# A four-layer graph network: a buffer for the last keys' adjacency, ScalarE in the late projections, and sums in one-bank tiles

## The chip, the core and the metric

One core of a Trainium2 chip runs one program. The metric is the device time of an execution in microseconds (us). The kernel before takes 3120.9 us, the median of 3 runs between 3119.28 and 3121.2 us.

The engines named below: TensorE (PE in the profile; PEld its weight loads), VectorE (DVE), ScalarE (ACT), GpSimd (POOL) and SyncE (SP). The last two mostly issue transfers here. Each engine works through a queue of its own in order, and waits where an instruction needs something of another engine or of a transfer.

## What is computed

Four layers stand on the same nodes: x is 2708 x 512, adj 2708 x 2708 with about 1% ones and a full diagonal, all in fp32. Each is `x = layernorm(x + layer(x))`. The change lies in layer 0:

```python
# layer 0, H = 4 heads of D = 128 features
Xw  = einsum('hnd,hde->hne', X by head, W)               # projection by head
f1, f2 = Xw @ V[:, 0], Xw @ V[:, 1]                      # two numbers per node and head
att = masked_softmax(sigmoid(f1 + f2.T) * adj, adj > 0)  # by head, n x n
Xc  = att @ Xw                                           # encoder
Xn  = batchnorm(Xc)
emb = batchnorm(elu(Xn @ Wm.T + bm) + Xn)                # mlp of the encoder
Y   = elu((att @ emb) @ W.T)                             # decoder, by head
out = batchnorm(elu(Y @ Wd.T + bd) + Y)                  # mlp of the decoder
```

Layer 1 is a mean over neighbours of `x @ W + b`, layer 2 an edge softmax times a node softmax, layer 3 an attention with the adjacency added to the scores twice. They follow in the same program, and the diff does not touch them.

## The kernel before

**Projection.** `project` takes the keys in blocks of 128 rows (22 blocks, `BLOCKS`, the last of 20). `values_of(jt)` multiplies block jt with all four heads' weights into a PSUM tile of two banks, `pxw`; its 512 wide part is copied to `xw` (L317, by ScalarE or VectorE, as the argument `scalar` says), and the column f2 is halved into `f2h` (L321, VectorE). The first 17 blocks are issued at once, with ScalarE for the first 14. The last five, 17 to 21, come in `rest`, which is called after the argument of step 1; ScalarE copies the first two of them. At the end of `rest` two small tiles are made: `bm1` (L343) and `enc_less` (L344).

**Encoder.** `encoder_pass` goes over 88 steps (`STEPS`): four parts of 22 blocks. A part is one half `hf` of the query nodes (1354 of 2708) and one pair `p` of heads; in order (0,0), (0,1), (1,0), (1,1). The block of 20 rows stands in the middle of a part, at place 11. For a step ScalarE makes two tanhs (L383, one for each head), VectorE joins them with the adjacency block `a` (`t`, 128 x 2708, the "argument", L378), ScalarE takes the exp (L515), and TensorE adds the result to 22 sums of up to 128 nodes each, 11 for a head (`node_sums`, L548; 44 records in the trace). The sums of three nodes share a bank with a column for the denominator each; the two heads use 4 banks each.

In the parts with p = 0 the block `a` comes from the input adjT (L480), VectorE turns zeros into -1e30 in two instructions (`mask_block`: z L443, a L444), and GpSimd writes the result to the DRAM tile `adj_d` (L448), from which the parts with p = 1 and the decoder load it. Steps up to a few are loaded ahead; `a` is a ring of 4 buffers (tag `a`). The block of 20 rows is not loaded as rows: its 20 x 1354 is cut into 4 strips of 384 columns, laid one below the other, with the gaps filled, by 7 transfers (`load_strips`, L430 to L435), into a buffer of the same ring; the strips of f1 go into `few` (L421).

**End of a part.** `keep` divides the sums by the denominators (rc L781, L782; rows L783, VectorE), and gives back two "turns", one for a head. A turn transposes the rows on TensorE (L802, L810) into banks, and the results are copied to `ft` (L823; columns 512, 512 and 330), by ScalarE or VectorE. The last bank also holds the transposed reciprocals; VectorE copies them to `sm`, 11 x 128 (L812), and GpSimd writes `sm` to the DRAM tile `rs_d` in two transfers (L814, L818). `sm` is taken from the pool `att` with the pool's own number of buffers, two. The turns are called within the first steps of the next part, and the exp of a step is issued behind the copies of the turn before it:

```python
if pending == 1:
    exponentials(k - 1, *copies_done)
```

**Mlp and decoder.** `mlp` normalises `ft` (L944, ScalarE, 452 or 450 columns each), multiplies four output groups in each of the six column chunks (L964), and applies elu (L701 ScalarE; L706, L708 VectorE), the sum with `ft` (L977) and statistics (L978). `decoder_pass` goes through the same four parts with the exps taken anew (L378, L635) or read back; its sums (`feature_sums`, L650) are six per part: two heads times three chunks of queries. At the end of a part VectorE reads them out (L1054).

**PSUM.** There are eight banks. For the encoder's sums they are eight tiles of one bank, four for a head; the turns of both heads transpose into the four of the second head (L802), so the next part's sums for that head start as these are copied out. The projection's, the decoder's six sums and the mlp's outputs use tiles of two banks with the tags `po0` to `po2`.

**Order.** The framework orders the instructions of each engine before the program runs, from the order they are written in, costs of its own and priorities; `behind(...)` adds a wish that one stands after another. It also places the waits: a tile's buffer is given to the next tile only after all its readers, transfers among them, are done. So a line moved, or a buffer fewer, can shift the place of others in the queues.

Of the kernel before, what the change touches and what calls it, by code (L numbers as in the profile page):

```python
# [29 lines left out]
def gnn_stack_kernel(  # L30
# [158 lines left out]
    with ExitStack() as l0:  # L189
# [45 lines left out]
        def project(att, psum):  # L235
# [66 lines left out]

            def values_of(jt, scalar):
                j0, n = BLOCKS[jt]
                pxw = psum.tile([P, H // HP, BANK], F32, tag=f"po{jt % HB}", name="pxw")
                pv = pxw[:, :, : HP * (P + 2)].rearrange("p a (k e) -> p a k e", k=HP)
                for h in range(H):
                    nc.tensor.matmul(
                        pv[:n, h // HP, h % HP, :],
                        xT_sb[:, h, j0 : j0 + n],  # L310
                        w0x[:, h, :],
                        start=True,
                        stop=True,
                    )

                copy = nc.scalar.copy if scalar else nc.vector.tensor_copy
                copy(  # L317
                    xw[:n, jt, :, :P].rearrange("p (a k) d -> p a k d", a=H // HP, k=HP),
                    pv[:n, :, :, :P],
                )  # L320
                nc.vector.tensor_scalar(  # L321
                    f2h[:n, jt, :].rearrange("p (a k) -> p a k", k=HP),
                    pv[:n, :, :, P + 1],
                    0.5,
                    None,
                    ALU.mult,
                )
            AT_ONCE = NT - 5
# [3 lines left out]
            def rest(step):  # L332

                with tc.issue_after(step.ins):
                    for jt in range(AT_ONCE, NT):
                        values_of(jt, jt < AT_ONCE + 2)
# [7 lines left out]
                    return nc.vector.tensor_scalar(  # L344
                        less, prm_sb[:, MB_ENC, :], 1.0, None, ALU.subtract
                    )

# [47 lines left out]
        def encoder_pass(values, att, banks, finish, f1b, blocks, spread, rest):  # L395

            FRONT, LEAD = 2, 2
            tanh, args, exps, tiles, loads, fetched, brought = ([] for _ in range(7))
# [65 lines left out]
            def bring(k):  # L464
# [6 lines left out]
                if k < len(blocks):  # L471
                    a = blocks[k]
                else:
                    a = att.tile([P, HW], F32, tag="a", name="a", bufs=4)
                    if n < P:
                        load_strips(a, src, hf)
                    else:
                        with behind(*[spread] if k < len(blocks) + 2 else []):
                            loads.append(
                                nc.sync.dma_start(a[:n, :w], src[j0 : j0 + n, h0 : h0 + w])  # L480
                            )
# [78 lines left out]
            for k in range(len(STEPS) + FRONT):  # L560
# [4 lines left out]
                if pending != 1 and 0 < k <= len(STEPS):  # L565
                    exponentials(k - 1)
                if inside and not pending:
                    form(k)
                    if k == 1:
                        args.append(rest(args[1]))  # L570
                        po = banks()
                if k >= FRONT:
# [32 lines left out]
        def decoder_pass(values, att, psum, finish):  # L605
# [53 lines left out]
            for part in PARTS:  # L659
                hf, p = part  # L660
                h0, w = HSPAN[hf]
                for place, jt in enumerate(ORDER):
# [20 lines left out]
                    if place == 0:  # L683
                        both = [
                            psum.tile([P, HP, BANK], F32, tag=f"po{q}", name="po", bufs=1)
                            for q in range(HB)
                        ]
                        po = [both[q][:, k, :] for k in range(HP) for q in range(HB)]
# [47 lines left out]
        with (  # L736
# [20 lines left out]
            def keep(hf, p, po, later):  # L757
# [35 lines left out]
                def turn(k, b, scalar, after):  # L793
# [15 lines left out]
                    if b + 1 == TURNS:  # L809
                        done = nc.tensor.transpose(bank[:NB, BANK - P :], rc, ident)  # L810
                        sm = att.tile([NB, P], F32, tag="sm", name="sm")
# [98 lines left out]
        with (  # L910
# [43 lines left out]
            for ci, (c0, w) in enumerate(CHUNKS):  # L954
# [3 lines left out]
                for o in range(C):  # L958
                    if o % HP == 0:
                        slot = (C * ci + o) // HP % HB  # L960
                        pair = psum.tile([P, HP, BANK], F32, tag=f"po{slot}", name="ps_mlp")
                    ps = pair[:, o % HP, :]
# [1314 lines left out]
```

## Time and profile before

| | us |
|---|---|
| median of 3 runs | 3120.9 |
| profiled execution | 3120.7 |
| its span, first to last instruction | 3118.8 |
| around the span | 1.9 |

The clock that TensorE was granted is 0.997 of full speed over the span. Where the stages lie, with the busy time of four engines in each:

| stage | us | PE | DVE | ACT | clock |
|---|---|---|---|---|---|
| projection | 0 to 41.7 | 32.1 | 21.9 | 22.2 | 1.00 |
| encoder, part 1 | 41.7 to 152 | 106.0 | 105.3 | 102.9 | 0.98 |
| first border | 152 to 165 | 11.2 | 12.7 | 10.6 | 1.00 |
| part 2 | 165 to 262 | 97.0 | 76.6 | 97.0 | 1.00 |
| second border | 262 to 278 | 13.5 | 15.7 | 12.3 | 0.89 |
| part 3 | 278 to 375 | 96.9 | 85.6 | 97.0 | 1.00 |
| third border | 375 to 388 | 11.3 | 12.9 | 10.4 | 1.00 |
| part 4 | 388 to 487 | 98.6 | 67.7 | 93.0 | 1.00 |
| last border, batch norm | 487 to 505 | 16.6 | 9.0 | 14.1 | 1.00 |
| mlp | 505 to 590 | 83.4 | 69.9 | 52.6 | 1.00 |
| decoder | 590 to 1030 | 435.7 | 306.8 | 324.9 | 0.99 |
| mlp of the decoder | 1030 to 1092 | 60.1 | 55.9 | 24.7 | 1.00 |
| layers 1 to 3 | 1092 to 3118.8 | 2008.3 | 1185.4 | 491.5 | 1.00 |

How to read it: busy time next to the length of the stage shows how much room an engine has left. An engine with room can still be late at one place, and the borders are such places: there the work of four engines depends on each other in a chain, while inside a part the next steps are prepared ahead. A gap of TensorE's is looked up in the list of what each engine waited for, which names the last instruction to come.

### The profile page before, as it was taken

The numbers are of one execution on the slowest core, as the hardware profiler recorded it, in microseconds if no ns is written. First come the engines' busy times: TensorE is split into PE (matmuls) and PEld (weight loads), VectorE is DVE, ScalarE is ACT, GpSimd is POOL, SyncE is SP. The second block draws the span as 40 slices with busy tenths as digits, with TensorE's granted clock in tenths as the row PEclk, the third lists the DMA queues.
The fourth block names the chain that finished last, engine by engine and source line by source line (L and its number), as shares of the span: only waits on it lengthen the run. The fifth ranks groups of instructions, "written<-read, shape, count | busy, mean of one in ns | idle before, by whom it ended". The sixth has DMA issues, their size and how long they took to land.

```text
span 3118.8 us, 39610 instructions
## 1 busy us (share of the span) xinstructions
PE 3070.6 (98%) x15144; PEld 2336.9 (75%) x15144; DVE 2025.3 (65%) x3804; ACT 1353.1 (43%) x1655; POOL 175.2 (6%) x301
## 2 busy tenths in 40 slices
PE   8999999999999999999999999999999999999999
PEld 7999996544444447875588887787778888888886
DVE  7988966785885783452366668677555555555565
ACT  7999998587767350001133334435211111111111
POOL 1111100000000000000111101000010000000000
PEclk9999999999999999999999999999999999999999
DMA  8987964266445315530254445566331111111110
GB/s 277 333 313 251 321 235 144 79 232 221 161 173 192 108 42 158 144 97 31 67 166 133 136 138 165 164 177 184 108 95 36 50 51 51 51 51 50 50 52 29
DMA packets 207228, 430.10 MB, mean 138 GB/s; under 512 B 22218, under 2 KB 137598, under 8 KB 201294
## 3 DMA queue, kind: packets, MB, share of 16 engines
q1 hardware_dynamic: 182774, 326.20, 34.0%
q0 software_dynamic: 24256, 101.35, 8.9%
q8 instruction: 119, 1.95, 0.3%
q14 instruction: 71, 0.58, 0.1%
q10 hardware_dynamic: 8, 0.02, 0.0%
HBM read 330.07 MB, written 95.87 MB: 137 GB/s over the span
## 4 chain that ended last, share of the span: by engine, by line
PE 79%; ACT 8%; DVE 8%; issue 3%; DMA 1%; SPq 0%; DVEq 0%; ACTq 0%; POOLq 0%
PE po L1728 21%; PE ps_s L1523 18%; PE po L650 9%; PE ps_nb L1326 7%; PE ps_wide L1376 5%; PE po L548 4%; ACT t L383 4%; ACT t L515 3%; DVE t L378 2%; PE ps_v L131 2%; PE ps_sup L1934 2%; PE ps_hid L131 2%; PE ps_dec L1093 2%; PE ps_mlp L964 1%; DVE a L444 1%
## 5 line engine op out<-in xcount | busy, mean ns | idle before, releaser
L378 DVE SCALAR_TENSOR_TENSOR t<-t,a 128x2708 f32<-128x2708 f32 (+1 forms) x152 | 443.8, 2922 | 166.1 <-ACT t L383 165.8
L548 PE MATMUL po<-xw,t 128*128 128x129 f32 (+2 forms) x3872 | 428.2, 277 | 11.8 <-DVE rc L781 4.9
L548 PEld LDWEIGHTS po<-xw,t 128*128 128x128 f32 (+2 forms) x3872 | 422.8, 189 | 16.4 <-issue 7.9
L383 ACT ACTIVATE t<-f1b,f2h 128x1354 f32<-128x1354 f32 x296 | 404.4, 1412 | 34.2 <-PE po L650 34.2
L1523 PE MATMUL ps_s<-q,hT 128*128 128x256 f32 (+1 forms) x1848 | 405.5, 372 | 0.0
L1728 PE MATMUL po<-sup,e 128*128 128x256 f32 (+1 forms) x1512 | 398.2, 384 | 5.6 <-DVE c L1809 2.8
L650 PE MATMUL po<-t,emb 128*128 128x452 f32 (+3 forms) x1056 | 399.1, 547 | 4.3 <-ACT t L635 4.2
L1523 PEld LDWEIGHTS ps_s<-q,hT 128*128 128x128 f32 x1848 | 339.5, 190 | 49.5 <-issue 5.1
L650 PEld LDWEIGHTS po<-t,emb 128*128 128x128 f32 (+1 forms) x1056 | 194.2, 191 | 202.1 <-issue 189.2
L1728 PEld LDWEIGHTS po<-sup,e 128*128 128x128 f32 (+1 forms) x1512 | 264.7, 185 | 59.6 <-issue 19.8
L1728 PE MATMUL po<-held,T 128*128 128x256 f32 x1200 | 293.8, 380 | 0.0
L1728 PEld LDWEIGHTS po<-held,T 128*128 128x128 f32 x1200 | 227.0, 190 | 31.1 <-issue 0.9
L2129 DVE SCALAR_TENSOR_TENSOR e<-a_cols,ps_s 128x512 f32<-128x512 f32 (+1 forms) x121 | 79.6, 658 | 233.8 <-PE ps_s L1523 229.9
L1523 PE MATMUL ps_s<-hT 128*128 128x256 f32 (+2 forms) x968 | 213.8, 372 | 0.8 <-ACT sup L1941 0.7
L515 ACT ACTIVATE t<-t 128x2708 f32<-128x2708 f32 x88 | 209.2, 2377 | 8.8 <-DVE t L378 8.1
L1523 PEld LDWEIGHTS ps_s<-hT 128*128 128x128 f32 x968 | 175.1, 190 | 29.1 <-issue 3.9
L1326 PE MATMUL ps_nb<-hid_hi,at 128*128 128x512 f32 x484 | 185.6, 390 | 0.4 <-DVE at L1318 0.4
L635 ACT ACTIVATE t<-t 128x2708 f32<-128x2708 f32 x64 | 157.3, 2458 | 60.4 <-DVE t L378 60.2
L1326 PE MATMUL ps_nb<-hid_lo,at 128*128 128x512 f32 x462 | 180.0, 390 | 0.0
L2031 ACT ACTIVATE a_score<-a_score,neg_big 128x512 f32<-128x512 f32 (+3 forms) x131 | 88.4, 683 | 196.0 <-DMA a_score<-in_adjT_dram 98.9
L2121 ACT ACTIVATE q<-ps_wide,uq 128x256 f32<-128x256 f32 (+1 forms) x44 | 20.5, 465 | 335.7 <-PE ps_wide L1376 335.7
L1633 ACT ACTIVATE e<-e 128x512 f32<-128x512 f32 (+1 forms) x187 | 113.8, 615 | 118.2 <-DVE e L1632 117.9
(276 smaller groups left out, 3995.4 us busy)
## 6 DMA issues: line engine op xcount, KB each, us to landing
a<-adj_d SPq DMA_DIRECT2D x113, 677.0 KB
a_cols<-in_adjT_dram SPq DMA_DIRECT2D x200, 256.0 KB
kept<-t POOLq DMA_DIRECT2D x20, 1354.0 KB, 8.4
t<-kept SPq DMA_DIRECT2D x20, 1354.0 KB
raw<-in_adjT_dram SPq DMA_DIRECT2D x105, 256.0 KB
a<-in_adjT_dram SPq DMA_DIRECT2D x37, 677.0 KB
adj_d<-a POOLq DMA_DIRECT2D x37, 677.0 KB, 6.2
a_score<-in_adjT_dram SPq DMA_DIRECT2D x55, 256.0 KB
```

Source lines behind the costliest of these rows:

```text
L131: nc.tensor.matmul(ps[:n], xt[:, c, :n], w[:, c, :], start=(c == 0), stop=(c == C - 1))
L378: return nc.vector.scalar_tensor_tensor(t, t, GUARD, ab, ALU.add, ALU.mult)
L383: done = nc.scalar.activation(t[:, k, :], f1b[k][:n, :w], AF.Tanh, bias=f2h[:n, jt, h : h + 1], scale=0.5,)
L515: nc.scalar.activation(t, t, AF.Exp, scale=0.5)
L548: nc.tensor.matmul(po[k][b][:m, s * DR : (s + 1) * DR], t[own : own + n, k, i0 : i0 + m], values[own : own + n, jt, HP * p + k, :], start= ...
L635: nc.scalar.activation(t, t, AF.Exp, scale=0.5)
L650: nc.tensor.matmul(po[HB * k + q][:, :qw], values[r : r + n, jt, h * P : (h + 1) * P], t[r : r + n, k, q0 : q0 + qw], start=(place == 0), ...
L1326: nc.tensor.matmul(pos[it][:n], at, half[:, jt, :], start=(jt == 0 and k == 0), stop=(jt == NT - 1),)
L1376: nc.tensor.matmul(ps[:, :width], w(c, o), xt(c), start=(c == 0), stop=(c == C - 1),)
L1523: nc.tensor.matmul(ps[:, jb, i:w], keys[:, c, j : j + P], st["q"][:, c, i:], start=(c == 0), stop=(c == C - 1),)
L1633: return nc.scalar.activation(e, e, AF.Exp)
L1728: nc.tensor.matmul(po[bank][rows, half, :], lhsT, rhs, start=(k == 0 and half == 0) if first is None else first, stop=last, skip_group_che ...
```

## The change

Four things, all in layer 0:

1. `values_of` and `rest`: of the late blocks 17 to 21 ScalarE copies three rather than two, and for those three it also writes the half of f2 (an activation, scale 0.5), which VectorE did. The exp of step 0 is issued after the last of these, rather than ahead of the argument of step 1.
2. The strips of the last block's adjacency get a tile of their own, `a_few` (one buffer, 384 columns), loaded at place 4 of each part behind the newest block load. The ring `a` is for full blocks alone.
3. `decoder_pass` and `mlp`: six tiles of one bank rather than three of two.
4. `sm` has one buffer rather than two.

```diff
--- before.py
+++ after.py
@@ -300,6 +300,8 @@
                 load_columns(NCH - 1)
                 nc.sync.dma_start(prm_sb, prm)
 
+            AT_ONCE, taken = NT - 5, []
+
             def values_of(jt, scalar):
                 j0, n = BLOCKS[jt]
                 pxw = psum.tile([P, H // HP, BANK], F32, tag=f"po{jt % HB}", name="pxw")
@@ -318,14 +320,13 @@
                     xw[:n, jt, :, :P].rearrange("p (a k) d -> p a k d", a=H // HP, k=HP),
                     pv[:n, :, :, :P],
                 )
-                nc.vector.tensor_scalar(
-                    f2h[:n, jt, :].rearrange("p (a k) -> p a k", k=HP),
-                    pv[:n, :, :, P + 1],
-                    0.5,
-                    None,
-                    ALU.mult,
-                )
-            AT_ONCE = NT - 5
+                half = f2h[:n, jt, :].rearrange("p (a k) -> p a k", k=HP)
+                if scalar and jt >= AT_ONCE:
+                    taken.append(
+                        nc.scalar.activation(half, pv[:n, :, :, P + 1], AF.Copy, scale=0.5)
+                    )
+                else:
+                    nc.vector.tensor_scalar(half, pv[:n, :, :, P + 1], 0.5, None, ALU.mult)
             for jt in range(AT_ONCE):
                 values_of(jt, jt < 2 * NT // 3)
 
@@ -333,7 +334,7 @@
 
                 with tc.issue_after(step.ins):
                     for jt in range(AT_ONCE, NT):
-                        values_of(jt, jt < AT_ONCE + 2)
+                        values_of(jt, jt < AT_ONCE + 3)
                     h0, w = HSPAN[1]
                     for q, (q0, _) in enumerate(HCH[1]):
                         f1_rows(HB + q, later_rows[:, q0:], q == 0)
@@ -341,9 +342,10 @@
                     copies(xw[:, NT - 1].rearrange("p h e -> p (h e)"))
                     copies(f2h[:, NT - 1, :])
                     nc.vector.tensor_scalar(bm1, prm_sb[:, MB_DEC, :], 1.0, None, ALU.subtract)
-                    return nc.vector.tensor_scalar(
+                    last = nc.vector.tensor_scalar(
                         less, prm_sb[:, MB_ENC, :], 1.0, None, ALU.subtract
                     )
+                return last, taken[-1]
 
             return f1b, blocks, spread, rest
 
@@ -395,7 +397,7 @@
         def encoder_pass(values, att, banks, finish, f1b, blocks, spread, rest):
 
             FRONT, LEAD = 2, 2
-            tanh, args, exps, tiles, loads, fetched, brought = ([] for _ in range(7))
+            tanh, args, exps, tiles, loads, fetched, brought, few = ([] for _ in range(8))
             state = {"f1b": f1b}
 
             def rows_of(k):
@@ -470,15 +472,18 @@
                 src = adjT if prepare else adj_d
                 if k < len(blocks):
                     a = blocks[k]
+                elif n < P:
+                    a = few.pop()
                 else:
                     a = att.tile([P, HW], F32, tag="a", name="a", bufs=4)
-                    if n < P:
-                        load_strips(a, src, hf)
-                    else:
-                        with behind(*[spread] if k < len(blocks) + 2 else []):
-                            loads.append(
-                                nc.sync.dma_start(a[:n, :w], src[j0 : j0 + n, h0 : h0 + w])
-                            )
+                    with behind(*[spread] if k < len(blocks) + 2 else []):
+                        loads.append(
+                            nc.sync.dma_start(a[:n, :w], src[j0 : j0 + n, h0 : h0 + w])
+                        )
+                if STEPS[k][1] == 4:
+                    few.append(att.tile([P, FEW], F32, tag="a_few", name="a_few", bufs=1))
+                    with behind(loads[-1]):
+                        load_strips(few[0], src, hf)
                 last_load[:] = loads[-1:]
                 if prepare:
                     mask_block(a, hf, jt, rows, width, *args[-1:])
@@ -562,13 +567,15 @@
                 copies_done = []
                 if inside:
                     open_step(k)
-                if pending != 1 and 0 < k <= len(STEPS):
+                if pending != 1 and 1 < k <= len(STEPS):
                     exponentials(k - 1)
                 if inside and not pending:
                     form(k)
                     if k == 1:
-                        args.append(rest(args[1]))
+                        done, scalar_done = rest(args[1])
+                        args.append(done)
                         po = banks()
+                        exponentials(0, scalar_done)
                 if k >= FRONT:
                     part, place = STEPS[k - FRONT]
                     t, _ = tiles[k - FRONT]
@@ -681,11 +688,10 @@
                         if p == 0 and jt in KEPT[1]:
                             count(hf, jt, att)
                     if place == 0:
-                        both = [
-                            psum.tile([P, HP, BANK], F32, tag=f"po{q}", name="po", bufs=1)
-                            for q in range(HB)
+                        po = [
+                            psum.tile([P, BANK], F32, tag=f"po{b}", name="po", bufs=1)
+                            for b in range(HP * HB)
                         ]
-                        po = [both[q][:, k, :] for k in range(HP) for q in range(HB)]
                     feature_sums(part, place, t)
                 later += finish(hf, p, po, rb) or []
             for work in later:
@@ -808,7 +814,7 @@
                     cw = min(w, c0 + BANK) - c0
                     if b + 1 == TURNS:
                         done = nc.tensor.transpose(bank[:NB, BANK - P :], rc, ident)
-                        sm = att.tile([NB, P], F32, tag="sm", name="sm")
+                        sm = att.tile([NB, P], F32, tag="sm", name="sm", bufs=1)
                         nc.vector.tensor_copy(sm, bank[:NB, BANK - P :])
                         full = (NB - 1) * P
                         nc.gpsimd.dma_start(
@@ -956,10 +962,8 @@
                     normal(ci + 1)
                 pss = []
                 for o in range(C):
-                    if o % HP == 0:
-                        slot = (C * ci + o) // HP % HB
-                        pair = psum.tile([P, HP, BANK], F32, tag=f"po{slot}", name="ps_mlp")
-                    ps = pair[:, o % HP, :]
+                    slot = (C * ci + o) % (HP * HB)
+                    ps = psum.tile([P, BANK], F32, tag=f"po{slot}", name="ps_mlp")
                     for c in range(C):
                         nc.tensor.matmul(
                             ps[:, :w],
```

Lines after the change stand 2 to 7 further down: L378 becomes L380, L515 L520, L548 L553, L812 L818, L823 L829, L650 L657.

## The prediction

> **What bounds the kernel.** I read the page's engine table first, then the groups, then TensorE's waits of the first 1100 us (the change ends there), then one window of the encoder, and last the timeline where the edits act.
>
> ```profile
> span 3118.8 us, 39610 instructions
> ...
> PE 3070.6 (98%) x15144; PEld 2336.9 (75%) x15144; DVE 2025.3 (65%) x3804; ACT 1353.1 (43%) x1655; POOL 175.2 (6%) x301
> ...
> L378 DVE SCALAR_TENSOR_TENSOR t<-t,a 128x2708 f32<-128x2708 f32 (+1 forms) x152 | 443.8, 2922 | 166.1 <-ACT t L383 165.8
> L548 PE MATMUL po<-xw,t 128*128 128x129 f32 (+2 forms) x3872 | 428.2, 277 | 11.8 <-DVE rc L781 4.9
> ...
> L515 ACT ACTIVATE t<-t 128x2708 f32<-128x2708 f32 x88 | 209.2, 2377 | 8.8 <-DVE t L378 8.1
> ```
>
> ```profile
> PE po L650 <- ACT t L635: 4.2, 4, 3.3
> PE po L548 <- ACT t L515: 3.9, 1, 3.9
> ...
> PE po L548 <- DVE enc_less L344: 1.5, 1, 1.5
> ...
> PE tp_emb L983 <- DVE ft L977: 1.4, 4, 0.6
> ```
>
> ```profile
> 130.00:260.00 130.00, 128.24 (x1172) 127.04 (x1171) 107.85 (x89) 127.20 (x82) 14.39 (x26) 1.00 0.88 327
> ```
>
> TensorE is 98% busy, so a gain can only be one of its gaps: the waits list (total, times, longest) names 3.9, 1.5 and some 1.4 us that the change touches. The third fence is decisive the other way: from 130 to 260 us ScalarE (fourth busy time) works 127.2 of 130 us, as hard as TensorE (128.2). A step of the encoder costs TensorE 4.91 us (44 records of L548) and ScalarE 4.98 us (distance of exps L515 from 174.72 to 199.62 us, five steps). So a delay of ScalarE inside a part is never made up, and reaches the end of the part whole.
>
> **Part one, the start (late projections on ScalarE).** The timeline has the last argument step L378 end at 37.99 and enc_less, which TensorE's first sum waits for, at 41.74. In between VectorE does three wide copies L317 (0.59 from start to start), four or five small ones (0.07 to 0.15), two f_later copies (0.59) and one wait. One wide copy and the halves of f2h go: 0.59 + 3 x 0.15 = 1.04. I take -1.1, bounds -1.5 (the whole wait) and 0. ScalarE gets 0.47 + 3 x 0.2 = 1.1 us ahead of exp 0 (35.13 to 36.2); that is hidden, since its exp 2 stands 2.2 us idle for VectorE; uncovered it would cost the 1.1 back.
>
> **Part two, the strips' own buffer.** In the old ring the load of a full block waits for the slot of a block behind:
>
> ```profile
> 94.95 0.87 DVE L443 TENSOR_SCALAR z<-a 128x1354 bf16<-128x1354 f32 x1 [1.70 <-DMA a<-in_adjT_dram]
> ...
> 97.33 2.97 DVE L378 SCALAR_TENSOR_TENSOR t<-t,a 128x2708 f32<-128x2708 f32 x1
> ...
> 100.34 2.46 ACT L515 ACTIVATE t<-t 128x2708 f32<-128x2708 f32 x1 [2.32 <-DVE t L378]
> ...
> 102.85 0.58 PE L548 MATMUL po<-xw,t 128*128 128x129 f32 x1 [3.92 <-ACT t L515]
> ```
>
> The bracket is the idle time before: 1.70 us of VectorE for a load issued at 87.46, right after a write of adj_d landed (87.41). With the strips out of the ring the load may use the slot freed at 79.84, so it is issued 7 us earlier and the wait goes: -1.75 (with its issue), bounds 0 (if another transfer takes the place) and -2.5. The 28 strip transfers are as many as before but earlier: seven issues of 0.36 us, 2.5 us of SP's queue per part, past which one block load is pushed; block loads here are issued 7 us ahead, so it is hidden. Parts one and two together: -2.85.
>
> **Part three, six one-bank tiles.** Decoder: the largest gap, 3.3 us at 793 us, ends with exp L635 (793.95 to 796.41; TensorE starts 796.44). The pair it would need is read out by 796.29, so freeing banks singly gains nothing: 0. One read-out now stands on VectorE ahead of an argument step; its bank is complete at 789.4, and VectorE is idle from 787.8 to 790.9, so that is hidden, and would cost 0.6 without the hole. Bounds -0.5 and +0.6. Mlp: the ScalarE order of the changed kernel puts five of the 21 normalisations (0.655 us from start to start) behind the first elu L701, so VectorE's chain, idle 5.3 us until then, starts 3.3 earlier. TensorE's gaps for ft there sum to 2.8 us in the timeline (the four in the list, 1.4, are the longest). I take -2.0, bounds -3.3 and 0.
>
> **Part four, sm in one buffer.** This is small in the diff and it decides. Head 1's sm (L812) now cannot be written before both rs_d writes of head 0's sm have landed, and the order of the changed program puts one more argument step ahead of it.
>
> ```profile
> DMA to landing us min/median/max: 1.6/4.1/7.8
> ```
>
> ```profile
> 387.58 0.27 DVE L812 COPY sm<-po 11x128 f32<-11x128 f32 x1
> 387.78 2.96 DVE L378 SCALAR_TENSOR_TENSOR t<-t,a 128x2708 f32<-128x2708 f32 x1
> 387.89 0.43 ACT L823 COPY ft<-po 128x330 f32<-128x330 f32 x1 [1.20 <-DVE sm L812]
> ...
> 388.22 2.46 ACT L515 ACTIVATE t<-t 128x2708 f32<-128x2708 f32 x1
> 388.38 5.40 PE L548 MATMUL po<-xw,t 128*128 128x129 f32 x46 [0.47 <-ACT ft L823]
> ```
>
> The first fence is the view of the tile sm (its eight pairs of writes), the second the timeline of the third border: sm at 387.58; 0.3 us later ScalarE's last ft copy, which waits for it; behind that in ScalarE's queue the exp of the next step, then all later tanhs. The same three start within 0.7 us of each other at the borders at 164, 277 and 388 us. Border one: sm moves behind the argument step (164.31 to 167.27), +3.0; writes landed at 165.8, in time. Border two: VectorE is busy throughout, the same 2.96 goes ahead of sm, +3.0. Border three: the writes land at 392.4 and 392.9 (7.7 us: a kept write of 1354 KB, issued at 381.92, is ahead of them in POOL's queue), so sm goes from 387.58 to 392.9, +5.3; bounds +3.0 (the argument step alone) and +5.3. The last border: second sm at 493.92, writes landed 493.75: +0.2. From this goes what the exps then had in hand, at most 0.1 at the ends of parts. Sum of the four: +11.4.
>
> On DMA, the Trainium skill (DMA: Bandwidth & Descriptors, "Anatomy of one DMA — SWDGE (gpsimd) path") gives a fixed cost of about 2.0 us per transfer, these being 5 KB. With that figure border three would be +3.0, the sum 2.3 us less; the trace's own 1.6 to 7.8 us decides.
>
> Who waits for whom else: TensorE needs the bank of that ft copy, but the new order has it 17 of 22 sums into the step rather than 7 to 12, so TensorE idles about 2, 2.5 and 4 us rather than 0 to 0.5. Idle time of 2.07 us (263.6 to 265.9) was followed by 3.4 us at half clock, 3.3 us at 793 by 6.8, 1.5 by none. Half of 3.4 is 1.7 us; of it about 1.3 is made up over 20 steps of 0.07 us, since TensorE then runs behind exps that are ready. Three borders at 0.4 to 0.7: +1.5, bounds 0 and +5.
>
> The skill's page TensorE: Matmul & The Clock Gate ("Why this matters for your kernels") asks for no gap over about 3 us; by it only border three pays, and the term would be about +0.5. The row at 263 us shows a shorter gap paying.
>
> **Sum.** -2.85 + 0 - 2.0 + 11.4 + 1.5 = +8.05 on the profiled execution: 3118.8 of span and 1.9 around it, 3120.7, gives 3128.75. The median of the runs is 0.2 above the profiled one, their spread 1.9. Forecast **3128.6**; its own range, from the bounds of border three and the clock, 3124 to 3133. A difference under 0.2% (6.2 us) could not be told from none.
>
> **Rivals.** (1) ScalarE passes sm: the copy finds its bank free without it, or sm slips in early, and the borders cost nothing. For it: at border two the bracketed wait is missing from the list for sm. Against: at all four borders the copy starts 0.03 us after sm's end. Gain: -2.85 - 2.0 and up to -2.4 for a gap at 265 us that the new order shortens: 3113.5. It is faster as soon as the borders cost less than 1 us together. Chance 0.11. (2) The borders cost one argument step each and no more, the writes land in time and the clock stays: 3 x 2.96 - 4.85 + 0.2 = +4.2, 3125; not slower by the bound. For it: writes landed after 1.6 us at 492. Chance 0.20. (3) The clock: each border's idle time brings 6.8 us at half speed as at 795 us, 2.9 us less work each, little made up: +4 to +6 over the forecast, 3134. For it 793 us; against 98 us, where 3.9 idle brought 3.4. Chance 0.13. (4) The gap at 793 us closes after all, with its slow clock: -3.3 - 3.0, 3122.3. Against: its exp keeps its place in ScalarE's order. Chance 0.06. The forecast keeps 0.50, of which a tenth lies within the bound. So faster 0.11, within 0.2% 0.20 + 0.06 + 0.05 = 0.31, slower 0.45 + 0.13 = 0.58. The range 3116 to 3135 leaves out most of rival 1 and the top of 3.
>
> **What would show it.** Argument L378 with no wait near 95 us and TensorE's first sum near 40.6: parts one and two. Sm's second copies behind an argument step, and the waits list with ft L829 after sm as a new top entry: part four; if the exp after each border stands less than 2.5 us later relative to the border's start, it is wrong. Gap at 793 us unchanged: part three. PE clock digits below 1 at the borders: the clock term. The forecast falls if the old ring's slots, and not sm, set ScalarE at the borders.

## The result, and the profile after

The changed kernel takes 3127.44 us (median of 12 runs, 3125.13 to 3129.1), the kernel before beside it 3118.86 us (12 runs, 3116.02 to 3121.6). The ratio is 1.0026 with a 95% interval of 1.0017 to 1.0035: slower by some 8.6 us. The profiled execution took 3126.81 us with a span of 3125.0, 6.1 us over the profiled one before.

Where the time goes is read from the start of the same sum on TensorE in both traces (every 44th record of the encoder, every 48th of the decoder), after minus before:

| place | after minus before, us |
|---|---|
| first sum of the encoder | -1.75 |
| step 12, behind the late block load | -3.42 |
| step 22, before the first border | -3.43 |
| step 43, before the second border | +0.92 |
| step 67, before the third border | +3.57 |
| last sum of the encoder | +6.83 |
| last sum of the mlp | +6.45 |
| decoder: 2/11, 5/11 and 1/2 through | +9.63, +8.75, +5.28 |
| last sum of the decoder | +6.45 |

So the encoder's first part gains 3.4, its three inner borders cost 4.35, 2.65 and 3.26, and the rest ends nearly even: the mlp takes 0.55 back, and the decoder moves up and down by some 3 us and ends where it began. ScalarE's exps (L515 before, L520 after), compared in the same way, shift by the same 4.35, 2.65 and 3.26 at the three borders: what the sums lose there is what the exps come late. The list of TensorE's waits in the first 1110 us (total, times, longest) has the new entry on top:

```profile
PE po L553 <- ACT ft L829: 6.2, 3, 2.7
...
PE po L657 <- ACT t L642: 4.5, 7, 2.0
PE po L553 <- DVE rc L787: 4.3, 3, 1.4
PE po L553 <- ACT t L520: 3.0, 2, 2.2
PE po L553 <- DVE enc_less L345: 1.9, 1, 1.9
...
PE tp_emb L987 <- DVE ft L981: 1.7, 2, 0.9
```

The first border in the timeline (start, us, engine and line; in brackets the idle time before and what ended it), in the kernel before:

```profile
161.23 2.96 DVE L378 SCALAR_TENSOR_TENSOR t<-t,a 128x2708 f32<-128x2708 f32 x1
...
164.11 0.27 DVE L812 COPY sm<-po 11x128 f32<-11x128 f32 x1
164.31 2.96 DVE L378 SCALAR_TENSOR_TENSOR t<-t,a 128x2708 f32<-128x2708 f32 x1
164.42 0.43 ACT L823 COPY ft<-po 128x330 f32<-128x330 f32 x1 [0.58 <-DVE sm L812]
```

In the changed kernel:

```profile
157.80 5.85 DVE L380 SCALAR_TENSOR_TENSOR t<-t,a 128x2708 f32<-128x2708 f32 x2
...
159.34 1.07 ACT L829 COPY ft<-po 128x512 f32<-128x512 f32 x2 [1.86 <-PE po L808]
...
165.03 0.28 DVE L818 COPY sm<-po 11x128 f32<-11x128 f32 x1 [1.38 <-DMA rs_d<-sm]
165.34 0.43 ACT L829 COPY ft<-po 128x330 f32<-128x330 f32 x1 [4.93 <-DVE sm L818]
...
165.67 2.46 ACT L520 ACTIVATE t<-t 128x2708 f32<-128x2708 f32 x1
...
165.83 3.59 PE L553 MATMUL po<-xw,t 128*128 128x129 f32 x16 [1.98 <-ACT ft L829]
```

The second and the third border of the changed kernel:

```profile
276.38 2.96 DVE L380 SCALAR_TENSOR_TENSOR t<-t,a 128x2708 f32<-128x2708 f32 x1
...
279.27 1.55 DVE L446 SCALAR_TENSOR_TENSOR a<-z,a 128x1354 f32<-128x1354 bf16 x1
...
280.75 0.27 DVE L818 COPY sm<-po 11x128 f32<-11x128 f32 x1
...
281.06 0.43 ACT L829 COPY ft<-po 128x330 f32<-128x330 f32 x1 [3.83 <-DVE sm L818]
```

```profile
388.13 5.85 DVE L380 SCALAR_TENSOR_TENSOR t<-t,a 128x2708 f32<-128x2708 f32 x2
...
394.41 0.28 DVE L818 COPY sm<-po 11x128 f32<-11x128 f32 x1 [0.43 <-DMA rs_d<-sm]
394.72 0.43 ACT L829 COPY ft<-po 128x330 f32<-128x330 f32 x1 [4.47 <-DVE sm L818]
```

Read them from the top. At the first and the third border two arguments now run together (x2, 5.85 us) where there was one ahead of sm and one behind. Then VectorE stands idle for another 1.38 or 0.43 us, ended by a transfer: the write of head 0's sm. All that time ScalarE waits (4.93 and 4.47 us) with the exp behind it. At the second border sm starts at 280.75, behind one argument more than before and the masks, with no idle time for the transfer (head 0's writes had landed at 277.50); ScalarE waits 3.83.

### The profile page after: what moved, and what is told of

It is laid out like the page before. It is cut to its first block, busy times and chain, and to the rows that moved or that the text cites. A ratio compares the mean times of both kernels' runs of the same rounds, so it can differ in the third digit from the quotient of the medians.

```text
span 3125.0 us, 39602 instructions
## 1 busy us (share of the span) xinstructions
PE 3072.0 (98%) x15144; PEld 2339.9 (75%) x15144; DVE 2024.7 (65%) x3800; ACT 1354.4 (43%) x1659; POOL 176.2 (6%) x301
## 4 chain that ended last, share of the span: by engine, by line
PE 77%; ACT 9%; DVE 8%; issue 4%; DMA 2%; POOL 0%; SPq 0%; DVEq 0%; ACTq 0%; POOLq 0%
PE po L1732 21%; PE ps_s L1527 19%; PE po L657 9%; PE ps_nb L1330 7%; PE ps_wide L1380 5%; ACT t L385 4%; ACT t L520 4%; DVE t L380 3%; PE ps_v L131 2%; PE ps_sup L1938 2%; PE ps_dec L1097 2%; PE ps_hid L131 2%; PE po L553 2%; PE ps_mlp L968 1%; PE ps_e L1660 1%
## 5 line engine op out<-in xcount | busy, mean ns | idle before, releaser
L380 DVE SCALAR_TENSOR_TENSOR t<-t,a 128x2708 f32<-128x2708 f32 x148 | 439.8, 2975 | 178.8 <-ACT t L385 178.5
L553 PE MATMUL po<-xw,t 128*128 128x129 f32 (+2 forms) x3872 | 431.9, 278 | 16.5 <-ACT ft L829 6.2
L553 PEld LDWEIGHTS po<-xw,t 128*128 128x128 f32 (+2 forms) x3872 | 423.7, 189 | 24.3 <-issue 8.3
L657 PE MATMUL po<-t,emb 128*128 128x452 f32 (+3 forms) x1056 | 397.5, 546 | 5.2 <-ACT t L642 4.5
L657 PEld LDWEIGHTS po<-t,emb 128*128 128x128 f32 (+1 forms) x1056 | 193.8, 190 | 202.6 <-issue 188.1
L520 ACT ACTIVATE t<-t 128x2708 f32<-128x2708 f32 x88 | 209.4, 2380 | 4.3 <-DVE t L380 3.5
```

Source lines behind the costliest of these rows:

```text
L380: return nc.vector.scalar_tensor_tensor(t, t, GUARD, ab, ALU.add, ALU.mult)
L520: nc.scalar.activation(t, t, AF.Exp, scale=0.5)
L553: nc.tensor.matmul(po[k][b][:m, s * DR : (s + 1) * DR], t[own : own + n, k, i0 : i0 + m], values[own : own + n, jt, HP * p + k, :], start= ...
L657: nc.tensor.matmul(po[HB * k + q][:, :qw], values[r : r + n, jt, h * P : (h + 1) * P], t[r : r + n, k, q0 : q0 + qw], start=(place == 0), ...
```

## The experiments

All ratios are to the kernel before, run on the same chip beside them. A ratio is estimated from all runs, so that it can differ from the quotient of the two medians by up to 0.0004; medians of different rows are best compared through their ratios.

| run | median, us | before, us | ratio | 95% interval |
|---|---|---|---|---|
| e1_sm_two | 3115.94 | 3120.01 | 0.9986 | 0.9977 to 0.9995 |
| e2_sm_one | 3129.52 | 3120.01 | 1.0030 | 1.0019 to 1.0041 |
| e3_banks | 3119.82 | 3120.01 | 1.0001 | 0.9992 to 1.0009 |
| e6_late | 3117.66 | 3120.01 | 0.9994 | 0.9985 to 1.0002 |
| e10_order | 3123.89 | 3119.05 | 1.0017 | 1.0008 to 1.0026 |
| e9_rs_sp | 3131.29 | 3119.05 | 1.0038 | 1.0026 to 1.0051 |
| e5_few | 3117.90 | 3119.05 | 1.0000 | 0.9991 to 1.0008 |
| e4_enc_sm_two | 3116.23 | 3119.05 | 0.9993 | 0.9983 to 1.0002 |
| e12_sm_behind | 3121.06 | 3119.47 | 1.0007 | 0.9999 to 1.0016 |
| e11_tanh | 3194.34 | 3119.47 | 1.0238 | 1.0225 to 1.0252 |

### Is it sm? Both ways round

e1_sm_two gives sm a second place: head 1's sm takes the tile of the f1 strips, which is free at the borders:

```diff
-                        sm = att.tile([NB, P], F32, tag="sm", name="sm", bufs=1)
+                        if k:
+                            sm = att.tile([P, HP, FEW], F32, tag="few", name="sm", bufs=1)[:NB, 0, :P]
+                        else:
+                            sm = att.tile([NB, P], F32, tag="sm", name="sm", bufs=1)
```

> The changed kernel, but head 1's sm in a buffer of its own (it borrows the tile of the f1 strips, free at the borders). Theory (one buffer of sm costs the borders 4.3 + 2.6 + 3.3 + 0.2 us, as the two traces show, and what is left is a small gain): 10 us less than the changed kernel, 3117, ratio to before 0.999 (0.998 to 1.000); the exp after each border starts within 1 us of where it stood relative to the border before. Rival (the borders are late for the strips' or the banks' sake, sm only happens to be there): the time stays at 3127, ratio 1.0026.

The other way round, the kernel before with this one line changed:

```diff
-                        sm = att.tile([NB, P], F32, tag="sm", name="sm")
+                        sm = att.tile([NB, P], F32, tag="sm", name="sm", bufs=1)
```

> The kernel before with nothing changed but one buffer for sm. Theory: all of the loss is here, +9 to +12 us, ratio 1.003 to 1.004, above what the whole change costs, since its gains are missing; each of three borders shows an argument step or a landing ahead of sm. Rival (ScalarE passes sm, or the loss needs the new order of the strips): within 0.05% of before.

Both came as the theory had it: ratio 0.9986 instead of 1.0026, and +9.5 us for the one line. In e1_sm_two the difference of the sums to before is the same on both sides of every border (-0.17 us at steps 22, 24 and 43, -0.16 at 45, -0.15 at 67, -0.14 at 68). Its waits of TensorE from 150 to 400 us:

```profile
PE po L553 <- DVE rc L787: 4.7, 3, 2.1
PE po L553 <- ACT ft L832: 0.9, 2, 0.5
```

The entry of 6.2 us is back at the 0.9 that the kernel before has. In e2_sm_one the exps come 2.89, 2.66 and 4.28 us later at the three borders. So sm is the loss, and the rest of the change is a gain of about 4 us by the medians: e1_sm_two is faster than both kernels. (Its trace shows less, since the profiled execution, 3118.98, is the slowest of its 11.)

### The argument ahead, or the landing?

One buffer brings two things: the scheduler puts an argument ahead of sm, and sm waits for the landing. e10_order has the first alone: two places for sm, but the turn is written behind the argument.

```diff
                     if turns:
+                        if inside and pending == 1:
+                            form(k)
                         scalar = pending == 1 or part[1] == 0
...
-                if inside and pending:
+                if inside and pending > 1:
```

> The changed kernel with two places for sm (as in e1_sm_two), but head 1's turn is written behind the next step's argument, so that VectorE has the order of the changed kernel without its wait for the writes. Theory (a border costs the argument step that is ahead, 2.96 us, and the landing only what comes on top): +3.0 us at the first and third border, +2.6 at the second, against e1_sm_two; sum +8.6, 3124.5, ratio to before 1.0015 (1.0005 to 1.0025). Rival (the landing alone makes the delay; the argument is moved into time that is lost anyway): within 2 us of e1_sm_two, 0.9990.

Measured 1.0017, as expected. Its first border:

```profile
156.88 5.84 DVE L380 SCALAR_TENSOR_TENSOR t<-t,a 128x2708 f32<-128x2708 f32 x2
...
162.65 0.27 DVE L823 COPY sm<-po 11x128 f32<-11x128 f32 x1
162.96 0.43 ACT L834 COPY ft<-po 128x330 f32<-128x330 f32 x1 [3.46 <-DVE sm L823]
```

The same two arguments, and sm directly behind them with no transfer in the bracket: ScalarE waits 3.46 us, 2.88 more than the 0.58 of the kernel before. From step 22 to the end of the encoder its sums go from -4.35 to +3.97 us against before: 8.3 us at three borders. The exps give 2.89, 2.65 and 2.77 for the single ones: an argument's 2.96 at each, less what the exps had in hand. The changed kernel has 1.46 more at the first border, none at the second and 0.49 at the third, close to what its sm waits there for the transfer (1.38, none, 0.43).

e9_rs_sp aims at the landing: SyncE issues the writes.

```diff
-                        nc.gpsimd.dma_start(
+                        nc.sync.dma_start(
```

(for both writes of sm)

> The changed kernel with one buffer for sm, its rs_d writes issued by SyncE instead of GpSimd. In this build the argument stays behind sm at the first and third border; sm still waits for the writes. Theory (what is left is the landing beyond the 3.1 to 3.8 us between the two sm): if SyncE's writes land in 2 to 5 us, each border costs 0 to 1.5 us, the second 2.6 (its argument is still ahead), sum 3 to 5, 3120, ratio 1.000 (0.999 to 1.001). Rival (any wait for a write at this place costs the 3 to 4 us seen, whoever issues it): 3127, 1.0026.

The theory's number fell: 3131.29, more than the changed kernel. The wait on the transfer is there, and longer:

```profile
157.95 1.31 SPq L820 DMA_DIRECT2D rs_d<-sm  x1
...
159.31 0.91 SPq L824 DMA_DIRECT2D rs_d<-sm  x1
...
165.18 0.28 DVE L818 COPY sm<-po 11x128 f32<-11x128 f32 x1 [4.77 <-DMA rs_d<-sm]
165.49 0.43 ACT L829 COPY ft<-po 128x330 f32<-128x330 f32 x1 [5.42 <-DVE sm L818]
...
165.98 4.24 PE L553 MATMUL po<-xw,t 128*128 128x129 f32 x18 [4.03 <-ACT ft L829]
```

With one argument fewer ahead of it sm still starts only at 165.18. SyncE issues the two writes 1.1 and 2.5 us after head 0's sm is done (GpSimd in the changed kernel: 0.3 and 0.8), and sm starts 5.9 us after the second issue (7.0 there): later issued and sooner done, it comes 8.6 us after head 0's sm rather than 8.1. So the two parts do not add up: sm goes when the later of the two is done. In the changed kernel the argument's 2.96 us lie inside the landing at the first and third border, and the landing adds 1.38 and 0.43 (the brackets above).

The exps come 4.84, 2.49 and 3.52 us later at the three borders, little more than in the changed kernel. The sums show 7.01, 0.33 and 6.01: at the first and the third border TensorE stood 4.0 us for the bank, 18 and 12 records into the step (32 in the changed kernel), and then had 6.8 us at half speed:

```profile
165.20:172.00 6.80, 6.02 (x28) 6.02 (x29) 4.20 (x3) 6.51 (x5) 0.00 (x0) 0.50 0.33 106
```

(the column behind POOL's busy time is the clock, 0.50.) The two together put the sums 2.2 and 2.5 us behind their exps; the first was made up by the second border, the other was not. It is what the prediction's third rival describes, and 2.5 of the 3.1 us by which the three borders cost more here than in the changed kernel.

### Through which wait does it reach the path?

e12_sm_behind keeps one buffer, but writes sm behind ScalarE's copy out of the same bank.

```diff
                         done = nc.tensor.transpose(bank[:NB, BANK - P :], rc, ident)
+                    dst = ft[:, h, h0 + c0 : h0 + c0 + cw]
+                    with behind(*after):
+                        copied = copy(dst, bank[:, :cw])
+                    if b + 1 == TURNS:
                         sm = att.tile([NB, P], F32, tag="sm", name="sm", bufs=1)
...
-                    dst = ft[:, h, h0 + c0 : h0 + c0 + cw]
-                    with behind(*after):
-                        copied = copy(dst, bank[:, :cw])
```

> The changed kernel, still one buffer for sm, but sm is written behind ScalarE's copy of 330 columns out of the same bank instead of ahead of it. Theory (the loss is ScalarE standing behind sm, through the bank that both read): the exps after the borders are no longer late; TensorE, which needs that bank 17 sums into the step, still waits for sm, 1 to 2.5 us at each of three borders, and makes up about 1.3 of it in each part: 0 to +4 us against e1_sm_two, 3118, ratio to before 0.9995 (0.9985 to 1.0008). Rival (the loss is the bank held for TensorE, and the exps are only late with it): as the changed kernel, 3127, 1.0026.

Measured 3121.06, ratio 1.0007: inside the expected range of the ratio, but +5.1 us against e1_sm_two, over the upper end that was expected there; and 6 us less than the changed kernel. The exps stand free at the first border (ScalarE's three copies in one row, the exp right behind), while VectorE stands 3.10 us for the transfer:

```profile
160.70 1.41 ACT L819 COPY ft<-po 128x512 f32<-128x512 f32 x3 [1.86 <-PE po L808]
162.15 2.46 ACT L520 ACTIVATE t<-t 128x2708 f32<-128x2708 f32 x1
...
168.10 0.28 DVE L822 COPY sm<-po 11x128 f32<-11x128 f32 x1 [3.10 <-DMA rs_d<-sm]
```

TensorE then waits for sm itself (`DVE sm L822`, 3.2 us, 2 times, in its list). The exps after the first border are 0.5 us earlier than ahead of it, and 0.6 later at the end of the encoder. The first border costs the sums 2.6 us here (-2.07 to +0.53), but they make it up, and by the end of the encoder, at -0.64, only 1.4 us of the three borders is left, where the changed kernel has 10.3. Most of the borders' loss therefore went through ScalarE's queue, and a smaller part through the bank. The whole program shows less of it, about half of the way from the changed kernel to e1_sm_two by the ratios: the trace of e12_sm_behind gains 1.4 us less ahead of the first border than the changed kernel, loses 0.8 at the last border, and gains nothing in the decoder, where that of e1_sm_two gains 1.7. Whether the first two belong to the edit or to the execution is not shown; the third is taken up below.

### The other three parts, each by itself

e6_late, the late projections on the kernel before (the main lines):

```diff
-                        values_of(jt, jt < AT_ONCE + 2)
+                        values_of(jt, jt < AT_ONCE + 3)
...
+                if scalar and jt >= AT_ONCE:
+                    taken.append(
+                        nc.scalar.activation(half, pv[:n, :, :, P + 1], AF.Copy, scale=0.5)
+                    )
...
+                        exponentials(0, scalar_done)
```

> The kernel before with the late projections alone (three copies and three halves on ScalarE). Theory: TensorE's first sum at 40.0 instead of 41.7 us, but the block load of the step near 97 us, unchanged in its ring, takes the 1.75 us back there, so that the sums stand less than 0.5 us from before at step 20: ratio 0.9998 to 1.0002. Rival (the start is worth its 1.75 us to the end): 0.9994, sums 1.7 us earlier at step 40.

e5_few, the strips' own buffer on the kernel before, with the second place for sm:

```diff
+                elif n < P:
+                    a = few.pop()
...
+                if STEPS[k][1] == 4:
+                    few.append(att.tile([P, FEW], F32, tag="a_few", name="a_few", bufs=1))
+                    with behind(loads[-1]):
+                        load_strips(few[0], src, hf)
```

> The kernel before with the strips' own buffer alone (two places for sm, as in e1_sm_two). Theory: the wait of 1.70 us for the block load at 95 us goes, and its sums stand 1.7 us earlier from step 12 to the end of the encoder: -1.7 us, 0.9995 (0.9988 to 1.0002). Rival (the load is late for another reason, or another load takes the place): no difference of the sums at step 20.

Neither differs from before by more than its interval; the traces say more. e5_few: the sums stand -0.10 us from before at step 11 and -1.78 at step 12, as expected, but -0.6 from step 22 on: 1.2 of the gain is gone by the end of the part. e6_late: the first sum is 1.91 us earlier; at steps 1 to 5 only 0.29 of it is left, after a clock window at half speed at 39.8 us, and 0.89 from step 22 to the end of the encoder (in between the difference moves from -1.7 to +0.6), more than the expected nothing and less than the rival's whole. Together the two gain more than these 1.5 us: seven traces have both, and in six of them the sums stand 2.1 to 4.4 us earlier at step 22 (in e1_sm_two, whose start was late, 0.2). Why they do not add up is not shown.

e3_banks, the one-bank tiles on the kernel before, and e4_enc_sm_two, which is e1_sm_two with the same edit backwards:

```diff
-                        both = [
-                            psum.tile([P, HP, BANK], F32, tag=f"po{q}", name="po", bufs=1)
...
+                        po = [
+                            psum.tile([P, BANK], F32, tag=f"po{b}", name="po", bufs=1)
...
-                        pair = psum.tile([P, HP, BANK], F32, tag=f"po{slot}", name="ps_mlp")
-                    ps = pair[:, o % HP, :]
+                    slot = (C * ci + o) % (HP * HB)
+                    ps = psum.tile([P, BANK], F32, tag=f"po{slot}", name="ps_mlp")
```

> The kernel before with the six one-bank tiles in decoder and mlp alone. Theory (the two decoder differences, a gap of 2.0 us at 655 us and the closed gap at 793 us, come from the new order of ScalarE and cancel; the mlp gains 0.5): -1 to +1 us, ratio 0.9997 to 1.0003, with the gap at 793 us closed and one near 650 us opened. Rival one (freeing banks singly is worth what closed at 793 us, 3.5 us, and the gap at 655 us comes from elsewhere): -4 us, 0.9987. Rival two (the first gap is the banks', the closed one is not): +3.5 us.

> e1_sm_two with the tiles of two banks again in decoder and mlp: the encoder's two parts alone. Theory (the tiles gain 3.3 us at 793 us and lose as much in new gaps at 648 us and after 805 us): within 1 us of e1_sm_two, ratio to before 0.9987. Rival (the tiles are a gain of some 2.5 us that e3_banks hid in its scatter): 2.5 us more than e1_sm_two, 0.9995.

e3_banks: ratio 1.0001, and its trace has both of the expected differences: TensorE's gap at 793 us is closed, and one of 2.0 us has opened at 647.7, with five of 0.3 to 0.5 between 804 and 829. At 793 us, e3_banks:

```profile
786.89 2.44 ACT L635 ACTIVATE t<-t 128x2708 f32<-128x2708 f32 x1
...
789.13 0.69 DVE L1051 SCALAR_TENSOR_TENSOR ot<-po,bn_scale,rb 128x452 f32<-128x452 f32 x1 [1.58 <-PE po L650]
...
793.58 3.06 DVE L1051 SCALAR_TENSOR_TENSOR ot<-po,bn_scale,rb 128x452 f32<-128x452 f32 x5
793.70 2.46 ACT L635 ACTIVATE t<-t 128x2708 f32<-128x2708 f32 x1 [0.41 <-DVE t L378]
794.32 4.06 PE L650 MATMUL po<-t,emb 128*128 128x452 f32 x10 [0.67 <-DVE ot L1051]
```

TensorE starts the new part at 794.32, while the exp that the wait list of before named runs until 796.16. So that exp was not what the first sums needed: they use the one of 786.89, and stood for the bank.

e1_sm_two and e4_enc_sm_two, with and without the tiles, have ratios of 0.9986 and 0.9993. The second lies nearer to the rival's 0.9995 than to the theory's 0.9987, but the intervals overlap, and e3_banks, 1.0001, shows no gain: the tiles are worth nothing that these runs can tell from none, and a gain of some 2 us is not excluded. The traces show why it is hard to see. From the first to the last sum of the decoder, against the one execution of before, six with one-bank tiles (the changed kernel, e1_sm_two, e3_banks, e9_rs_sp, e10_order, e12_sm_behind) have 0.0 three times and -1.7 three times, the four with two banks (e2_sm_one, e4_enc_sm_two, e5_few, e6_late) -1.0 to -1.6. The two groups with one-bank tiles differ by one clock window behind the gap of 2.0 us (last section).

### An attempt at the gap that the tiles open

```diff
-                tanhs(t, f1b, hf, p, jt, rows, w)
+                with behind(*exped[-1:]):
+                    tanhs(t, f1b, hf, p, jt, rows, w)
...
-                nc.scalar.activation(t, t, AF.Exp, scale=0.5)
+                exped.append(nc.scalar.activation(t, t, AF.Exp, scale=0.5))
```

> e1_sm_two, and in the decoder the two tanhs of a step are asked to stand behind the exp of the step before. Theory (the gap of 2.0 us at 648 us comes from a third tanh that the one-bank build's order puts ahead of an exp): the gap goes, -1.8 us against e1_sm_two, ratio to before 0.998. Rival (the early tanhs fill ScalarE's idle time elsewhere, and without them exps come late at other places): +1 us or more against e1_sm_two, with more time in the wait of the decoder's sums for exps than the 4.5 us of the changed kernel.

The rival held, and far beyond its number: 3194.34, 78 us more than e1_sm_two. From 590 to 1200 us TensorE waits

```profile
PE po L658 <- ACT t L643: 39.9, 19, 3.3
PE ps_y L1087 <- DVE ot L1075: 10.5, 3, 4.1
```

In the decoder some blocks are read back instead of computed; the likely reading, not tested by itself, is that the tanhs run ahead in that time, and that without this lead TensorE waits for the chain of tanh, argument and exp of each step. Its trace also has 58 us at half speed in the decoder, where that of before has 6.8. What in the order opens the gap at 648 us stays open: a third tanh ahead of the exp is what the timeline shows, and forbidding it everywhere cost far more than it could bring.

## Why the prediction was right, and where its terms were off

**Sm in one buffer** (forecast +11.4): right in mechanism and place, and in the size of the whole. Measured at the four borders, by the second sm less the shift that stood there: +4.35, +2.65, +3.26, +0.21, sum 10.5; forecast +3.0, +3.0, +5.3, +0.2. That the whole came so near is partly luck. At the first border the forecast had the writes land in time; they came 1.38 us after the argument. At the third it had 5.3 us for the landing, which came 2 us sooner. The landing differs from run to run: the first border's writes took 7.1 us (4.7 before), the third's 5.9 (7.8 before). The forecast took each border's landing from its one execution, while its own view of sm spans 1.6 to 7.8. That the argument and the landing do not add up was used rightly at the third border; e10_order and e9_rs_sp show it. With the fixed cost of about 2.0 us that the Trainium skill gives a transfer (DMA: Bandwidth & Descriptors, "Anatomy of one DMA — SWDGE (gpsimd) path"), an estimate would have put the first and the third border at 3.0 each. The traces of the changed kernel have 5.7 to 7.1 us for head 0's writes at these two, so the measurement decides against it here.

**Start and strips** (forecast -2.85): -3.43 at the first border. The start gave -1.75 for -1.1, the strips -1.67 for -1.75. The start was mis-sized (a quarter of a microsecond beyond its bound of -1.5); it also moves by itself between executions (below). The forecast, as the profile, names enc_less as what the first sum waits for. In all twelve traces the sum starts 0.15 us after the end of the last f_later copy (L288; before 41.59 and 41.74), and enc_less ends within 0.002 us of the sum's start, in most of them at it or after it. So the copy is the likelier release; the size does not hang on it.

**Mlp** (forecast -2.0): -0.55 in the changed kernel, -0.56 in e3_banks. This is the term most in error. The elu chain does start 3.3 us earlier, as forecast (VectorE's first L706 8.98 us after the first L964 before, L712 5.70 after L968 now), but TensorE's waits for ft did not shrink: four listed gaps of 1.4 us became two of 0.86 and 0.80, at other places. All its idle times ahead of `tp_emb`, the short ones too, sum to 1.65 us in the trace of before and 1.79 after, so the forecast's 2.8 us to be gained is not there. Where the 0.55 came from is not shown.

**Decoder** (forecast 0): the net is 0.0 (+6.44 at its first sum, +6.45 at its last), but the step to it was wrong. The forecast put TensorE's 3.3 us at 793 down to the exp that ended 0.03 us before it; the bank pair was free 0.15 us before it, and of the two only the bank was needed at once, as e3_banks shows. The gap closed, as the fourth rival had it, and the new order gave the same time back elsewhere, at 655 us (2.0 us and a clock window at 657.8) and after 813. That the net is exactly nothing is luck as well: without that window it is -1.7 in three other traces.

**The clock** (forecast +1.5): TensorE stood 1.98, 2.66 and 1.51 us at the three borders (forecast about 2, 2.5 and 4). Windows of 3.4 us at half speed came at 166.3 and 282.4 us, behind the first two, and none at the third border. Their cost does not show: the borders cost the sums what the exps come late, 4.35, 2.65 and 3.26. At the first border the sums stand at +0.55 at step 25, less than the exps' +0.92, and only drift up to +0.92 in the part. The term was 0 here; e9_rs_sp shows gaps of 4.0 us at which it was not.

**The sum** was +8.05 on the profiled execution and came out at +6.1; terms: 10.5 for 11.4, -3.43 for -2.85, -0.55 for -2.0, 0 for 0, 0 for +1.5. The medians of 12 runs moved by 8.6: the profiled execution before is 1.8 us over its median, the one after 0.6 under. So the forecast of 3128.6 is near the measured 3127.44 also because errors cancel: the terms were 1.9 us too high on the profiled pair, and the pair moved 2.5 us less than the medians.

## What to carry to other kernels

A buffer taken away from a small tile can cost what its slowest reader takes, and a store to DRAM is a reader: look who stands behind the next writer of that tile on its engine, and who stands behind that. The delay is the later of the new wait and of what the scheduler puts in front of the waiting instruction, so try the two apart before adding them. When a wait names an instruction that ended just before, look for others that ended as close: only the one whose result is used at once can be the cause.

## What the runs showed of the hardware

The two writes of an sm (10 rows and part of one, 5.4 KB together) landed 1.5 to 8.8 us after their issue by GpSimd; head 0's at the first border took 4.7 in one execution and 7.1 in another. Issued by SyncE they brought sm no sooner: 8.6 us from one sm to the next at the first border against 8.1, and 7.1 against 6.9 at the third.

The same program text reaches its first encoder sum at different times. With the start of before, three other traces have it 0.11 and 0.02 us earlier and 1.35 later (e2_sm_one). With the changed start it was 1.2 to 2.7 us earlier than before in seven traces, and 1.52 later in e1_sm_two. In the two late ones TensorE waited 3.2 and 2.0 us for xT_sb, and the clock was at half speed for 3.4 us from 34.9 us. The changed start alone thus spans 4.2 us in a program of 3120, before any of the work in question.

The same gap of 2.0 us, near 650 us in the decoder with one-bank tiles, was followed by 3.4 us at half speed in the traces of the changed kernel, e9_rs_sp and e12_sm_behind, and by none in those of e1_sm_two, e3_banks and e10_order. The ten us behind it in the changed kernel and in e1_sm_two (mean clock behind POOL's busy time):

```profile
656.98:666.98 10.00, 10.00 (x22) 5.00 (x23) 9.87 (x7) 5.97 (x4) 0.00 (x0) 0.83 0.62 206
```

```profile
649.85:659.85 10.00, 10.00 (x27) 5.07 (x28) 9.79 (x7) 7.67 (x6) 0.00 (x0) 1.00 0.64 207
```

Against the first sum of the decoder the sums behind it stand 3.19 to 3.21 us later than before in the first three traces and 1.50 to 1.51 in the others. So the window cost 1.7 us, half its length, and the difference is still there at the decoder's last sum.

The gap of 3.3 us near 793 us, with two-bank tiles, was followed by half speed for 6.8 us in the trace of before, for 3.4 us in those of e2_sm_one, e4_enc_sm_two and e5_few, and by none in e6_late. The mean clock from 790 to 830 us, in the order before, e2_sm_one, e6_late:

```profile
790.00:830.00 40.00, 36.70 (x90) 17.99 (x89) 37.63 (x38) 32.17 (x24) 0.00 (x0) 0.91 0.46 155
```

```profile
790.00:830.00 40.00, 36.70 (x93) 17.92 (x93) 33.69 (x32) 35.24 (x25) 0.00 (x0) 0.96 0.38 131
```

```profile
790.00:830.00 40.00, 35.75 (x93) 17.11 (x92) 40.00 (x41) 33.88 (x24) 0.00 (x0) 1.00 0.47 160
```

One step of the decoder behind the gap the sums had gained 1.1 to 1.2 us on before where the window was 3.4 us and 2.8 where there was none; two steps behind it, 1.1 to 1.2 and 1.5. So what a gap costs in clock is not read from its length in one trace: the same gap was followed by different windows, and a window's cost stays or is partly made up by what limits the stage next.
